# Softmax normalised in front of the transposes instead of behind the context, in a fused attention and feed-forward kernel

## The chip, the core and the metric

The kernel runs on one core of a Trainium2 chip, in one launch. The metric is the device time of that launch in microseconds. A core has five engines that run side by side, each with its own in-order instruction queue: TensorE (PE; its weight loads, PEld, overlap its matmuls), VectorE (DVE), ScalarE (ACT), GpSimd (POOL) and SyncE (SP, which here only issues DMAs). They meet at semaphores. TensorE writes to PSUM, the accumulation memory; everything else lies in SBUF.

## The reference

The whole computation has four layers over 8 batches of a 512 x 512 array: a step of a partial differential equation on a grid, a transformer block with adaptive layer norm, an expert feed-forward layer, and a gated low-rank response. The change lies in the attention of the transformer block. With B = 8, S = 512, 16 heads of 32 columns, and float32 throughout:

```python
x = _ln(src) * (1.0 + scale) + shift          # src: result of the grid step
q = (x @ Wq + bq)   # and k, v alike, split into 16 heads of 32
scores = einsum('bhqd,bhkd->bhqk', q / sqrt(32), k) + attention_bias
scores = where(src_mask, -inf, scores)
probs = softmax(scores, axis=-1)
ctx = einsum('bhqk,bhkd->bhqd', probs, v)
x = x + (ctx @ Wo + bo)
h = _ln(x) * g2 + beta2
x = x + _gelu2(h @ W1 + b1) @ W2 + b2
```

The bias is a full array of 8 x 16 x 512 x 512 values, 134 MB, and is read once.

## The kernel before

The kernel has three stages. `grid_stage` does the grid step of batch 0 and prepares coefficients. `attention_stage` does the attention of all 8 batches and, spread through it, the grid step of batches 1 to 7. `mlp_stage` does the rest; it begins near 1,110 us. The change touches `attention_stage` alone.

**Units.** The attention is cut into 128 units (b, c, r): batch b, group c of four heads, and r, one of four sets of 128 query rows. Within a batch I write t = 4c + r, from 0 to 15. A unit has four score tiles of 128 queries x 512 keys, one for each of its heads, and two bias tiles `bt` of two heads each (index u = 0 for heads 0 and 1, u = 1 for heads 2 and 3). The bias tiles come from memory three units ahead (`load_bias`), GpSimd adds the mask to them one unit ahead (`add_mask`), and the softmax is done in place in them. So a `bt` tile holds first the bias, then the negated scores, then the exponentials.

**What one pass of the loop does.** In pass i three units are in flight: `now` = unit i, `old` = unit i-1, `two` = unit i-2.

- `scores(i)` was issued at the end of pass i-1: four matmuls into four PSUM tiles s0 to s3, one buffer each.
- `values(two)` runs in passes where the unit two back has odd r: probabilities transposed earlier (`pt`), times v, into `ctx`. So it stands in front of the transposes of units with even t.
- For u = 0 and 1: `turned(old, u)` transposes two heads of the unit before, four 128 x 128 blocks each, into PSUM tiles `tr`, of which there are two, and copies each out as `pt`, on VectorE or ScalarE by a list written out by hand (`early`). Then `softmax(now, u)`: VectorE joins score and bias, negated, and takes the row minimum `mn` in one instruction, and ScalarE makes the exponential with the row sum in `sums`. Then one step of a job.
- Jobs (`fill`) are the projections of q, k, v and o, the transposes of the normalised input (`x1_in`) and back (`x1_back`), and the conversion of masks. For t = 0, 4, 8, 11 the job is a q block, for 1, 5, 9, 13 a k block, for 2, 3, 6, 7 an o block, for 10, 12, 14, 15 a v block. q and o are moved out of PSUM by VectorE, k and v by ScalarE.
- After the jobs are drained, `divide` follows in every fourth pass (t = 1, 5, 9, 13 of the running unit), then `inverse(old)`, then the grid sums of this pass and their loads, then `scores(i+1)`.

**The division before.** `inverse(old)` takes the reciprocals of four row sums (`rs`, 128 x 4) and spreads each over 32 columns on ScalarE (`rw`, 128 x 128). Once four units of a head group are through, `divide` transposes the four `rw` on TensorE (`rb`), ScalarE moves that to SBUF (`rbs`), and VectorE multiplies the context by it on its way out of PSUM (`ct`).

**The grid sums.** VectorE does up to three sums or products of 128 x 1024 per pass, by a table written out by hand (`GRID`); a `|` in it parts what comes ahead of `divide` from what comes behind. `grid_gate` makes GpSimd wait, at the start of the next pass, for the last grid operation on VectorE before it adds the next mask.

**Order.** Nearly every instruction is emitted under `keep_in_program_order` (`pin`), so that each engine's queue has the order of the emitting code. An instruction that waits holds up all that stands behind it on its engine.

Of the kernel before, what the change touches and what calls it, by code (L numbers as in the profile page):

```python
# [11 lines left out]
F32 = mybir.dt.float32  # L12
# [4 lines left out]
ALU = mybir.AluOpType  # L17
# [4 lines left out]
S = 512  # L22
D = 512
P = 128
R = 4
NH = 16
HD = 32
# [517 lines left out]
def attention_stage(  # L545
# [12 lines left out]
    nc = tc.nc  # L558
    with ExitStack() as ctx:
        wp = ctx.enter_context(tc.tile_pool(name="aw", bufs=1, reuse_waits="tile"))  # L560
        pp = ctx.enter_context(tc.tile_pool(name="ap", bufs=2, reuse_waits="tile"))
        ps = ctx.enter_context(tc.tile_pool(name="a_ps", bufs=1, space=PSUM, reuse_waits="tile"))

        pin = tc.keep_in_program_order
# [4 lines left out]
        def tp(out, src):  # L569
            pin(nc.tensor.transpose(out, src, ident))  # L570
# [20 lines left out]
        def mask_out(b, r):  # L591
            m = pp.tile([P, S], BF16, name=f"mk_{b}_{r}", tag=f"mk{r}", bufs=1)
            pin(nc.scalar.activation(m, mask[b, r], AF.Copy, scale=NEG))
            mask[b, r] = m

        def load_mask(b, r):
            mask_in(b, r)
            mask_out(b, r)
# [16 lines left out]
        def x1_back(b, r):  # L615
            tr = ps.tile([P, KC, P], F32, name=f"xb_{b}_{r}", tag="tr", bufs=2)
            for c in range(KC):
                tp(tr[:, c, :], x1s[b, c][:, r::R])
            pin(
                nc.vector.tensor_tensor(  # L620
                    xt[b][:, r, :], tr.rearrange("p c f -> p (c f)"), bo, ALU.add
                )
            )
# [43 lines left out]
        def v_block(b, m, tag="m", bufs=1):  # L667
            pr = ps.tile([P, D], F32, name=f"pv_{b}_{m}", tag=tag, bufs=bufs)
            half = block(
                pr,  # L670
                lambda k: x1s[b, k][:, m * P : (m + 1) * P],
                lambda k: w["Wv"][:, k, :],
            )
            yield half(0)
            yield half(1)
            t = io.tile([P, D], F32, name=f"v_{b}_{m}", tag=f"v{m}", bufs=2)
            pin(nc.scalar.copy(t, pr))
            vs[b, m] = t
# [155 lines left out]
        def grid_sums(n, j, late=True, early=True):  # L834
            ops = GRID.get(j, "")
            if "|" in ops and not (late and early):
                ops = ops.split("|")[late]
            elif not late:
                ops = ""
            for op in ops.replace("|", "").split():  # L840
                if op == "hh":
                    grid_ghosts(n)
                else:
                    grid_op(n, op)
# [7 lines left out]
        def grid_step(i, f):  # L852
            for n in range(1, NB):
                j = i - (16 * (n - 1) - 8)
                if -2 <= j <= 16:
                    f(n, j)
# [50 lines left out]
        def grid_early(j):  # L907
            grid_sums(1, j)
            grid_loads(1, j)

        def fill(b, t):

            n = b + 1
            jobs = []
            if b == 0:
                if t == 0:
                    homes = (("m", 1), ("tr", 2), ("tr", 2), ("ctx", 1))
                    for m in range(4):
                        jobs.append(v_block(0, m, *homes[m]))
                        jobs.append(grid_early(j) for j in (m + 3,))  # L920
                    jobs.append(grid_early(7) for _ in range(1))
                    jobs.append(mask_out(0, r) for r in (2, 3))
                elif t == 2:
                    jobs.append(add_bv() for _ in range(1))
                elif t in (3, 4, 7, 8):
                    jobs.append(x1_back(0, (3, 4, 7, 8).index(t)) for _ in range(1))
            if n == NB:
                at = dict(q=(0, 4, 9), k=(1, 6, 10), o=(2, 3, 7, 8))
                for key, f in (("q", q_block), ("k", k_block)):
                    if t in at[key]:  # L930
                        jobs.append(f(b, at[key].index(t) + 1))
                if t in at["o"]:
                    jobs.append(o_block(b - 1, at["o"].index(t)))
            elif t in (0, 4, 8):
                jobs.append(q_block(b, t // 4 + 1))
            elif t in (1, 5, 9):
                turn = (lambda c: x1_in(n, c)) if t == 9 else None
                jobs.append(k_block(b, t // 4 + 1, turn=turn))
            elif t in (2, 3, 6, 7):
                if b:  # L940
                    jobs.append(o_block(b - 1, (2, 3, 6, 7).index(t)))
            elif t == 11:
                jobs.append(q_block(n, 0))
            elif t == 13:
                jobs.append(k_block(n, 0))
            else:
                jobs.append(v_block(n, (10, 12, 14, 15).index(t)))
            if n < NB:
                if t in (11, 12, 13, 14):
                    jobs.append(x1_back(n, t - 11) for _ in range(1))  # L950
                if t >= 12:
                    jobs.append(load_mask(n, t - 12) for _ in range(1))
            elif t == 8:
                jobs.append(head_stats() for _ in range(1))
            elif t in (10, 11):
                jobs.append(head_norm(r) for r in (2 * t - 20, 2 * t - 19))
            elif t >= 12:
                jobs.append(head_turn(t - 12) for _ in range(1))
            for j in jobs:
                yield from j  # L960


        bias, ss, sums = {}, {}, {}
        pts, ctxs = {}, {}
# [86 lines left out]
                        k == 0, k == KC - 1,  # L1051
                    )

        def inverse(b, c, r):
            rs = small.tile([P, 4], F32, name=f"rs_{b}_{c}_{r}", tag="rs")
            pin(nc.vector.reciprocal(rs, sums.pop((b, c, r))))
            rw = pp.tile([P, 4, HD], F32, name=f"rw_{b}_{c}_{r}", tag="rw", bufs=4)
            pin(nc.scalar.copy(rw, rs[:, :, None].to_broadcast([P, 4, HD])))
            sums["w", b, c, r] = rw

        def divide(b, c):
            rb = ps.tile([P, R, P], F32, name=f"rb_{b}_{c}", tag="tr", bufs=2)
            for r in range(R):
                tp(rb[:, r, :], sums.pop(("w", b, c, r)).rearrange("p h d -> p (h d)"))
            rbs = pp.tile([P, S], F32, name=f"rbs_{b}_{c}", tag="rbs", bufs=1)
            pin(nc.scalar.copy(rbs, rb.rearrange("f r p -> f (r p)")))
            ct = pp.tile([P, S], F32, name=f"ct_{b}_{c}", tag="ct", bufs=5)
            pin(
                nc.vector.tensor_tensor(
                    ct, ctxs.pop((b, c)).rearrange("f r p -> f (r p)"), rbs, ALU.mult  # L1070
                )
            )
            cts[b, c] = ct

        def drain(jobs):
            for _ in jobs:
                pass
# [28 lines left out]
        for i in range(n + 2):  # L1106
            now = units[i] if i < n else None
            old = units[i - 1] if 1 <= i <= n else None
            two = units[i - 2] if i >= 2 else None
            jobs = fill(now[0], 4 * now[1] + now[2]) if now else iter(())  # L1110
            grid_gate(i)
            if i + 1 < n:
                add_mask(*units[i + 1])
            grid_step(i - 1, grid_pow)
            pair = two and two[2] % 2 == 1
            if pair:
                values(two[0], two[1], two[2] // 2)
            for u in range(2):
                if old:
                    turned(*old, u)  # L1120
                if now:
                    softmax(*now, u)
                next(jobs, None)
            drain(jobs)
            split = pair and two[2] == R - 1
            if split:
                grid_step(i, lambda n, j: grid_sums(n, j, late=False))
                divide(two[0], two[1])
            if old:
                inverse(*old)  # L1130
            if i + 3 < n:
                load_bias(*units[i + 3])
            if now and now[0] == NB - 1:
                head_load(4 * now[1] + now[2])
            if now and now[0] and now[1:] == (2, 1):
                nc.sync.dma_start(x1d[now[0] - 1], xt[now[0] - 1])
            grid_step(i, lambda n, j: grid_sums(n, j, early=not split))
            grid_step(i, grid_loads)
            if i + 1 < n:
                scores(*units[i + 1])  # L1140
# [821 lines left out]
```

## Time and profile before

| | |
|---|---|
| time, median of 3 runs | 2741.48 us (2741.33 to 2741.9) |
| the profiled execution | 2742.26 us, its span 2740.5 us |
| mean granted TensorE clock in the span | 0.994 |
| PE busy in the span | 2697.7 us (98%) |
| DVE, ACT, POOL busy in the span | 1910.8, 1030.4, 1501.5 us |
| one attention batch of 16 units (batches 1 to 6) | 125.8 us |
| ACT: one exponential of 128 x 512 | 715 ns |
| POOL: one mask addition of 128 x 1024 | 2141 ns |
| `rb` transposes on PE, 128 of them | 273 ns each (median) |
| `rw` and `rbs` copies on ACT | 297 and 570 ns (medians) |

A line of the timeline in the profile gives the start in us from the span's start, the length, the engine, the line of the kernel, the operation, the tiles written and read (out<-in, buffer numbers left out), the shape, and how many such instructions were put together (x4). Square brackets at its end tell how long the engine stood idle before it and what ended that. A line of a group of instructions gives the busy time, the mean duration in ns, and the idle time before them. L567 and L570 are the helpers `mm` and `tp`, through which all matmuls and transposes of this stage go; so they are told apart by their tiles. Matmuls overlap one another, so the durations of single ones add up to more than the time they take.

### The profile page before, as it was taken

The page shows a single profiled execution, that of the slowest core. Times are in us where ns is not written, and L with a number is a line of the kernel's source. Part 1 is how long each engine was busy: PE and PEld are TensorE (multiplying, and loading weights), DVE is VectorE, ACT ScalarE, POOL GpSimd, SP SyncE. Part 2 cuts the span into 40 slices and gives each one's busy share as a digit, 9 for nine tenths or more (in the row PEclk, how much of TensorE's full clock was granted, in tenths as well). Part 3 has the DMA queues.
Part 4 walks back from the last instruction along what each step waited for, and adds up shares of the span by engine and source line. Part 5 has one row for each costly group of instructions (what it writes and reads, how often), then busy time and mean ns, then how long its engine had stood idle before and what let it go on. Part 6 is the DMA issues. An engine that isn't in the chain of part 4 may idle for free.

```text
span 2740.5 us, 39851 instructions
## 1 busy us (share of the span) xinstructions
PE 2697.7 (98%) x14662; PEld 2008.0 (73%) x14662; DVE 1910.8 (70%) x3514; ACT 1030.4 (38%) x2189; POOL 1501.5 (55%) x1090
## 2 busy tenths in 40 slices
PE   7999999999999999999999999999999999999998
PEld 4455555555555555788888888888888888888887
DVE  7888888888888756577656756655456566565665
ACT  2566776766676766211211211211121221221221
POOL 3455555555555653565566555655636546546543
PEclk9999999999999999999999999999999999999999
DMA  8765767666676554642533443353133143142120
GB/s 314 241 204 178 242 188 239 204 217 222 196 235 192 166 156 158 192 123 41 161 127 73 124 144 100 79 163 118 58 127 116 58 158 116 59 158 100 58 77 31
DMA packets 190208, 405.27 MB, mean 148 GB/s; under 512 B 24024, under 2 KB 28704, under 8 KB 183742
## 3 DMA queue, kind: packets, MB, share of 16 engines
q1 hardware_dynamic: 186202, 391.97, 42.8%
q0 software_dynamic: 3360, 10.68, 3.1%
q8 instruction: 117, 1.92, 0.3%
q14 instruction: 77, 0.63, 0.1%
q10 hardware_dynamic: 452, 0.07, 0.0%
HBM read 366.97 MB, written 31.50 MB: 145 GB/s over the span
## 4 chain that ended last, share of the span: by engine, by line
PE 95%; DVE 3%; DMA 1%; issue 0%; ACT 0%; SPq 0%; ACTq 0%; POOL 0%; DVEq 0%; POOLq 0%
PE u L1177 28%; PE y L1177 28%; PE tr L570 8%; PE s L567 6%; PE ctx L567 4%; PE o L567 4%; PE pq L567 4%; PE pk L567 4%; PE pv L567 4%; PE btr L1180 1%; PE l L251 1%; DVE bt L1005 1%; PE rb L570 1%; PE xb L570 1%; PE ytr L1180 1%; DMA a<-in_A 0%
## 5 line engine op out<-in xcount | busy, mean ns | idle before, releaser
L982 POOL TENSOR_TENSOR bt<-bt,mk 128x1024 f32<-128x1024 f32 x256 | 542.6, 2141 | 56.8 <-DMA bt<-in_bias 47.3
L1177 PE MATMUL y<-wo,act 128*128 128x256 f32 x2560 | 572.8, 380 | 0.0
L1177 PEld LDWEIGHTS y<-wo,act 128*128 128x128 f32 x2560 | 481.5, 190 | 69.9 <-issue 6.7
L1010 ACT ACTIVATE bt<-bt,mn 128x512 f32<-128x512 f32 x512 | 365.6, 715 | 84.0 <-DVE mn L1005 83.1
L570 PEld LDWEIGHTS tr<-ident,bt 128*128 128x128 f32 x2048 | 228.7, 141 | 147.1 <-issue 114.1
L1005 DVE CUSTOM_DVE_ANT_0 bt<-s,bt 128x512 f32<-128x512 f32 x512 | 330.7, 683 | 1.3 <-PE s L567 1.3
L1177 PE MATMUL u<-bt,wi 128*128 128x256 f32 x1440 | 330.5, 379 | 0.0
L1183 DVE TENSOR_TENSOR act<-u,u 128x512 f32<-128x512 f32 x256 | 173.2, 686 | 210.3 <-PE u L1177 132.6
L1177 PEld LDWEIGHTS u<-bt,wi 128*128 128x128 f32 x1440 | 273.5, 190 | 37.2
L570 PE MATMUL tr<-ident,bt 128*128 128x128 f32 x2048 | 275.5, 277 | 7.5 <-ACT pt L1037 4.1
L1177 PE MATMUL u<-tb,ws 128*128 128x256 f32 x1024 | 242.2, 379 | 0.0
L1177 PE MATMUL y<-t,s 128*128 128x256 f32 x1024 | 234.2, 380 | 0.0
L1037 ACT COPY pt<-tr 128x512 f32<-128x512 f32 x306 | 172.8, 581 | 156.1 <-PE tr L570 152.8
L1186 POOL TENSOR_TENSOR t<-wo,t 128x512 f32<-128x512 f32 x64 | 106.6, 1682 | 200.5 <-PE y L1177 200.5
L1035 DVE COPY pt<-tr 128x512 f32<-128x512 f32 x206 | 141.7, 688 | 105.4 <-PE tr L570 97.1
L1177 PEld LDWEIGHTS u<-tb,ws 128*128 128x128 f32 x1024 | 194.3, 190 | 26.6 <-DVE tb L1183 0.2
L1177 PEld LDWEIGHTS y<-t,s 128*128 128x128 f32 x1024 | 191.1, 190 | 24.1
L1497 ACT ACTIVATE act<-act,b 128x512 f32<-128x512 f32 x128 | 82.9, 711 | 293.0 <-DVE act L1183 293.0
L1497 ACT ACTIVATE act<-act,bi 128x512 f32<-128x512 f32 x128 | 83.8, 712 | 282.6 <-DVE act L1183 282.6
L1183 DVE TENSOR_TENSOR x<-y,x 128x512 f32<-128x512 f32 (+1 forms) x97 | 64.6, 679 | 161.2 <-PE y L1177 107.3
L567 PE MATMUL s<-kt,qt 32*128 32x512 f32 x1024 | 173.7, 643 | 3.4 <-DVE mn L1005 2.5
L1183 DVE TENSOR_TENSOR u<-u,u 128x512 f32<-128x512 f32 x192 | 131.1, 683 | 57.9 <-PE u L1177 57.8
(325 smaller groups left out, 4252.3 us busy)
## 6 DMA issues: line engine op xcount, KB each, us to landing
bt<-in_bias SPq DMA_DIRECT2D x256, 512.0 KB
wo<-in_W SPq DMA_DIRECT2D x32, 1024.0 KB
wi<-in_Wi SPq DMA_DIRECT2D x32, 1024.0 KB
wo<-in_Wo_e SPq DMA_DIRECT2D x32, 1024.0 KB
wi<-in_W SPq DMA_DIRECT2D x28, 1024.0 KB
gq<-coef_q SPq DMA_DIRECT2D x21, 512.0 KB
x1d<-x SPq DMA_DIRECT2D x8, 1024.0 KB
x<-x1d SPq DMA_DIRECT2D x8, 1024.0 KB
```

Of the source, the lines that this page charges most:

```text
L567: pin(nc.tensor.matmul(out, lhsT=lhsT, rhs=rhs, start=start, stop=stop))
L570: pin(nc.tensor.transpose(out, src, ident))
L982: nc.gpsimd.tensor_tensor(bt, bt, mask[b, r][:, None, :].to_broadcast([P, 2, S]), ALU.add)
L1005: nc.vector.tensor_tensor_reduce(bt[:, i, :], ss[h], bt[:, i, :], -1.0, 3.0e38, ALU.add, ALU.min, mn)
L1010: nc.scalar.activation(bt[:, i, :], bt[:, i, :], AF.Exp, bias=mn, scale=-1.0, accum_out=sums[b, c, r][:, h : h + 1],)
L1035: pin(nc.vector.tensor_copy(pt[:, :, r % 2, :], tr))
L1037: pin(nc.scalar.copy(pt[:, :, r % 2, :], tr))
L1177: pin(nc.tensor.matmul(out, lhsT=lhsT, rhs=rhs, start=start, stop=stop))
L1180: pin(nc.tensor.transpose(out, src, idn))
L1183: pin(nc.vector.tensor_tensor(out, x, y, op))
L1186: pin(nc.gpsimd.tensor_tensor(out, x, y, op))
L1497: nc.scalar.activation(acts[g][:, k, :], acts[g][:, k, :], func, bias=bi[:, j : j + 1])
```

## The change

The row sums are applied to the exponentials themselves, in place, before they are transposed. `inverse` is called twice per unit, for heads 0 and 1 and for heads 2 and 3, now for the running unit `now` and no longer for `old`: the first call right behind the drained jobs, the second behind the grid sums. Each call makes the reciprocal of two sums on VectorE, multiplies the first of the two heads on ScalarE (128 x 512, a scale per row), and the second on GpSimd (128 x 512). `divide` becomes `context`: the transposes `rb`, the copies `rw` and `rbs` and the product are gone, and VectorE copies the context out of PSUM as it is. Apart from this, the four jobs of batch 0 that turn the normalised input back (`x1_back`) come at t = 3, 4, 6 and 7 in place of 3, 4, 7 and 8.

```diff
@@ fill
-                elif t in (3, 4, 7, 8):
-                    jobs.append(x1_back(0, (3, 4, 7, 8).index(t)) for _ in range(1))
+                elif t in (3, 4, 6, 7):
+                    jobs.append(x1_back(0, (3, 4, 6, 7).index(t)) for _ in range(1))
@@ attention_stage
-        def inverse(b, c, r):
-            rs = small.tile([P, 4], F32, name=f"rs_{b}_{c}_{r}", tag="rs")
-            pin(nc.vector.reciprocal(rs, sums.pop((b, c, r))))
-            rw = pp.tile([P, 4, HD], F32, name=f"rw_{b}_{c}_{r}", tag="rw", bufs=4)
-            pin(nc.scalar.copy(rw, rs[:, :, None].to_broadcast([P, 4, HD])))
-            sums["w", b, c, r] = rw
-
-        def divide(b, c):
-            rb = ps.tile([P, R, P], F32, name=f"rb_{b}_{c}", tag="tr", bufs=2)
-            for r in range(R):
-                tp(rb[:, r, :], sums.pop(("w", b, c, r)).rearrange("p h d -> p (h d)"))
-            rbs = pp.tile([P, S], F32, name=f"rbs_{b}_{c}", tag="rbs", bufs=1)
-            pin(nc.scalar.copy(rbs, rb.rearrange("f r p -> f (r p)")))
+        def inverse(b, c, r, u):
+
+            rs = small.tile([P, 2], F32, name=f"rs_{b}_{c}_{r}_{u}", tag="rs")
+            pin(nc.vector.reciprocal(rs, sums[b, c, r][:, 2 * u : 2 * u + 2]))
+            bt = bias[b, c, r, u]
+            pin(nc.scalar.mul(bt[:, 0, :], bt[:, 0, :], rs[:, 0:1]))
+            pin(nc.gpsimd.tensor_scalar(bt[:, 1, :], bt[:, 1, :], rs[:, 1:2], None, ALU.mult))
+
+        def context(b, c):
             ct = pp.tile([P, S], F32, name=f"ct_{b}_{c}", tag="ct", bufs=5)
-            pin(
-                nc.vector.tensor_tensor(
-                    ct, ctxs.pop((b, c)).rearrange("f r p -> f (r p)"), rbs, ALU.mult
-                )
-            )
+            pin(nc.vector.tensor_copy(ct, ctxs.pop((b, c)).rearrange("f r p -> f (r p)")))
             cts[b, c] = ct
@@ the loop
             drain(jobs)
+            if now:
+                inverse(*now, 0)
             split = pair and two[2] == R - 1
             if split:
                 grid_step(i, lambda n, j: grid_sums(n, j, late=False))
-                divide(two[0], two[1])
-            if old:
-                inverse(*old)
+                context(two[0], two[1])
             if i + 3 < n:
                 load_bias(*units[i + 3])
...
             grid_step(i, lambda n, j: grid_sums(n, j, early=not split))
+            if now:
+                inverse(*now, 1)
             grid_step(i, grid_loads)
```

## The prediction

> **What bounds the kernel now.** I read the page's chain first, then busy time by stage, then the timeline at one hand-over between units.
>
> ```profile
> PE 95%; DVE 3%; DMA 1%; issue 0%; ACT 0%; SPq 0%; ACTq 0%; POOL 0%; DVEq 0%; POOLq 0%
> ...
> 217.33:343.10 125.77, 125.53 (x818) 69.19 (x817) 110.37 (x238) 87.09 (x207) 71.63 (x51) 1.00 0.66 211
> 343.10:468.87 125.77, 125.52 (x817) 69.18 (x816) 109.75 (x237) 87.56 (x209) 71.68 (x51) 1.00 0.65 212
> ```
>
> The chain is TensorE. The stretches are two batches of attention, 16 units each (columns: length, then busy time of PE, weight loads, DVE, ACT, POOL, then the clock, DMA share and rate). Batches 1 to 6 repeat alike and PE is busy for all but 0.25 us: fewer PE instructions shorten a batch, and any wait put before PE lengthens it. ACT and POOL have room in sum, DVE less. So it matters when each result is there. Unit t=1 hands over to t=2:
>
> ```profile
> 357.55 1.22 DVE L695 TENSOR_TENSOR x<-x,gf 128x1024 f32<-128x1024 f32 x1
> 357.68 0.60 PE L570 MATMUL rb<-ident,rw 128*128 128x128 f32 x4
> 357.77 0.71 ACT L1010 ACTIVATE bt<-bt,mn 128x512 f32<-128x512 f32 x1
> 358.21 1.14 PE L567 MATMUL s<-kt,qt 32*128 32x512 f32 x8
> 358.48 0.67 ACT L661 ACTIVATE kt<-pk,bqk 128x512 f32<-128x512 f32 x1
> 359.05 0.57 ACT L1066 COPY rbs<-rb 128x512 f32<-128x512 f32 x1
> 359.28 1.09 PE L570 MATMUL tr<-ident,bt 128*128 128x128 f32 x8
> 359.65 0.69 DVE L1069 TENSOR_TENSOR ct<-ctx,rbs 128x512 f32<-128x512 f32 x1 [0.88 <-ACT rbs L1066]
> 360.67 1.07 ACT L1037 COPY pt<-tr 128x512 f32<-128x512 f32 x2
> 361.93 1.04 PE L570 MATMUL tr<-ident,bt 128*128 128x128 f32 x8
> ```
>
> PE issues the scores of unit 2 (s) and 1.07 us later the transposes (tr) of unit 1's heads 0 and 1. Their exponentials are long done, but ACT is still on the unit's last one. After an even unit the values (ctx) come between, and the transposes start 2.94 after the scores. Heads 2 and 3 follow at 3.72 (odd) or 5.58 (even).
>
> **The change, part by part.** *Removed:* 128 rb transposes; four stream in 0.44 us (unit t=1 takes 8.71, the like unit t=15 without rb 8.27), so 32 x 0.44 = 14 us of PE's path. ACT loses 128 rw copies (0.29) and 32 rbs copies (0.57), 55 us beside PE. The context copy stays at 0.69 on DVE, without its 0.88 wait.
>
> *Added, in sums:* 128 more reciprocals (two small ones per unit, some 0.09 each in DVE's queue, 11 us of its slack); 256 multiplies on ACT at the exponential's 0.72, 184 us, which makes 103 of 126 in a batch; 256 on POOL. All would hide by busy time.
>
> POOL's price has no like row:
>
> ```profile
> L1186 POOL TENSOR_TENSOR ws<-w 128x512 f32<-128x512 f32 x3 | 3.8, 1274 | 0.1
> L319 POOL COPY zi<-ident 128x128 f32<-128x128 f32 x1 | 0.3, 292 | 0.1
> L320 POOL TENSOR_SCALAR zi<-ident 128x128 f32<-128x128 f32 x1 | 0.6, 562 | 0.0
> ```
>
> The copy carried to 512 columns gives 0.6, the tensor_scalar 1.57; the two-input form at the right size is 1.27. The Trainium skill, "GPSIMD Engine Reference", section 3.1, puts a tight loop over 512 elements at 769 ns. I take 0.9, below the two-input row since one operand less is read, and keep 0.6 and 1.57: 29 us a batch on POOL, 101 of 126.
>
> *Waits, heads 0 and 1.* The first `inverse` stands behind the drained jobs, so ACT's multiply of head 0 queues behind the last exponential and behind what jobs leave on ACT (kt, v, mask). At t=1: kt is through at 359.05, the multiply ends at 359.77, PE sees it some 0.15 later (mn to s shows 0.14 to 0.18): 359.92 in place of 359.28, though PE, without rb, would be ready at 358.84. At t=3 the reciprocal waits for DVE's add of o (start 0.71 after the scores), the multiply runs 0.91 to 1.63, PE starts at 1.78 in place of 1.07. At t=15 v and mask go first: 345.65 for 344.17. After even units the 1.87 us of values cover all this; without that cover it would cost the like again.
>
> *Head 1 and the shared port.* The grid sums stand right behind the reciprocal on DVE, with both inputs in SBUF:
>
> ```profile
> 362.96 4.23 POOL L982 TENSOR_TENSOR bt<-bt,mk 128x1024 f32<-128x1024 f32 x2
> 366.32 1.95 DVE L695 TENSOR_TENSOR x<-x,gc 128x1024 f32<-128x1024 f32 x1
> ```
>
> This one takes 1.95 in place of 1.22, as if it began when POOL ended (367.19). So DVE's first sum (1.1) goes ahead of POOL's multiply, and the multiply ahead of the second sum: at t=3 POOL runs 1.9 to 2.8, and PE, wanting head 1 at 2.2, waits 0.7 more.
>
> *Heads 2 and 3.* The second reciprocal is behind all grid sums. ACT's multiply of head 2 waits for it, and the evictions of heads 0 and 1 (pt) are queued behind that multiply; PE needs their two PSUM buffers for heads 2 and 3. Where DVE evicts head 0 instead, that copy stood behind the grid sums before too and loses nothing but the port's time. At t=1: sums and reciprocal done at 362.2, multiply to 362.9, eviction to 363.5, so PE gets its buffer at 363.65; it wanted it at 362.53. At t=3 this adds 0.4.
>
> *Given back.* At t=2 and 6 DVE is 1.13 late for the next scores now (eight scores matmuls spread over 2.28 in place of 1.14); a PE that is already late hides that.
>
> *Net per unit, the saving of rb included.* t=1 and 5: heads 2 and 3 start 1.72 late, which covers DVE's 1.13, so 0.56 each remains. t=3: 0.71 (head 0) + 0.72 (head 1) + 0.4 (buffer) = 1.85. t=7: DVE has statistics there, [...]so only POOL's mask add (to 1.21) is in the way: 0.71 + 0.04 + 0.25 = 1.0. t=9: the last exponential ends 2.16 ahead of the scores, heads 0 and 1 come in time, and the buffers cost 0.55. t=11: one sum only, 0.71 + 0.72 = 1.4. t=13: kt and mask on ACT put PE's start from 329.02 to 329.72, POOL adds 0.35: 1.05. t=15: 1.5. Even units: 0. Sum 8.5 a batch, 51 for batches 1 to 6. Batch 7 has no grid sums (no port wait), and PE is idle there for 7.3 us of 125 already, which takes up a part: 4. Batch 0 is uneven, with DVE late in it: 4, guessed from the others' half. Total +59. With POOL at 0.6 the units 3, 11 and 13 lose some 0.8: 7.7 a batch, +54. At 1.57 heads 1 and 3 are 0.67 later at the seven odd units up to t=13: 13.2 a batch, +93 with the end batches in step.
>
> *The rest.* The add of the mask moves behind POOL's two multiplies: about 1 later, where the next unit reads it 1.5 to 6 later; at 1.57 that cover wears through at places. relu and its row transfer on ACT's queue come at most 0.72 later, and nothing waits for them before the next grid step. Bias loads on SP keep their order, three units ahead, and wait for buffers as late as PE itself is. Batch 0's turns (8 transposes and two adds moved one unit ahead, no DMA): t=8 has a 1.8 gap in front of one now, t=7 is tight itself; -3 to +2, I take 0.
>
> *The clock.*
>
> ```profile
> 92.50:95.90 3.40, 2.00 (x5) 0.68 (x4) 3.37 (x7) 1.48 (x2) 0.67 (x2) 1.00 1.04 400
> 133.40:136.80 3.40, 1.50 (x13) 1.04 (x11) 3.40 (x7) 1.31 (x4) 0.60 (x2) 1.00 0.43 120
> 136.80:143.60 6.80, 6.80 (x32) 3.15 (x36) 6.73 (x12) 3.97 (x11) 3.76 (x2) 0.50 0.29 97
> ```
>
> The Trainium skill, "TensorE: Matmul & The Clock Gate", Part 1, lets the clock halve after an idle window of about 3.4 us; by it these stalls cost nothing more. The trace is stricter: 1.50 busy of 3.40 was followed by half clock, 2.00 was not. My stalls leave PE 1.9 to 2.4 of 3.4 in their windows (t=15: 3.4 - 1.5; t=3: 3.4 - 1.43), between the two or above, and a stall is often split over two windows. I take 0; a halved window costs 1.7, three a batch over seven batches 36.
>
> **Sum.** The profiled execution took 2742.3 (span 2740.5 and 1.8 around it), 0.8 above the median 2741.5. 2742.3 + 59 - 0.8 = 2800.
>
> **Rivals.** (1) Everything hides: the multiplies reach PE before 1.07. Then rb's 14 goes, and some of the 18 of t=2 and 6: 2715 to 2727, faster. For it: room on ACT and POOL, sums of heads 0 and 1 ready 1 to 3 us ahead. Against: the order on ACT. It would need head 0's multiply to end by 0.9 after the scores, that is to stand before the last exponential, which the code doesn't do: 0.05. (2) The waits only eat the saving, within 5 of 2741: 0.03. (3) Waits half of mine, POOL not held by the port: 6 to 40, near 2765: 0.10. (4) My forecast, 40 to 75: 0.50. (5) POOL at 1.57, or half clock: heads 1 and 3 become the last, 93 in all, with the clock's 36 near 130: 2816 to 2870. For it: the only tensor_scalar row of POOL; against: that is one row, beside small sums of DVE: 0.32.
>
> A measurement here tells 0.2% (5.5 us) from no change. Faster 0.05, same 0.03, slower 0.92. The range leaves out (1), (2) and the ends: 2762 to 2868.
>
> **What would show it.** PE instructions 128 fewer; PE idle in front of tr, released by ACT bt and POOL bt, at odd units and not at even ones; batches of 134 in place of 125.8; POOL's multiply often near 2 by the port; clock 1.00. Wrong: batches under 126, or waits at even units, or halved clock throughout.

## The result, and the profile after

| | before | after |
|---|---|---|
| median of four runs each, side by side | 2741.69 us (2741.33 to 2744.88) | 2964.6 us (2959.65 to 2966.65) |
| the profiled execution, and its span | 2742.26, 2740.5 us | 2962.91, 2961.1 us |
| mean granted TensorE clock in the span | 0.994 | 0.970 |
| one attention batch, batches 1 to 5 | 125.8 us | 155.6 and 158.4 us, in turn |
| batch 6 | 125.8 us | 149.5 us |

The ratio is 1.0809, interval 1.0796 to 1.0822: 223 us slower. The forecast was 2800, with 2762 to 2868 around it. The direction was right and the size was not. Batches 1 to 6 make 178 of the 223, batch 0 makes 23 and batch 7 makes 19.

The page of the changed kernel, its busy times and its chain by engine:

```profile
PE 2757.7 (93%) x14534; PEld 2019.1 (68%) x14534; DVE 1964.3 (66%) x3642; ACT 1148.0 (39%) x2285; POOL 2012.7 (68%) x1346
...
PE 73%; POOL 12%; DVE 8%; issue 4%; ACT 2%; DMA 1%; SPq 0%; ACTq 0%; POOLq 0%; DVEq 0%
```

PE has 128 instructions fewer (14,534 for 14,662), as the rb transposes are gone; it is nevertheless busy 60 us longer, which the slower clock does: without POOL's multiplies (an experiment below, clock 0.992) the same instructions keep it busy 2682.1 us. In the chain POOL has gone from 0 to 12%, DVE from 3 to 8%. ACT, which got as many multiplies as POOL, has 2%.

Two batches in busy time by stage (columns: length, then busy PE, weight loads, DVE, ACT, POOL, then clock, DMA share and rate):

```profile
240.50:396.13 155.63, 132.55 (x801) 69.60 (x800) 118.19 (x254) 101.82 (x220) 138.38 (x84) 0.95 0.53 171
396.13:554.53 158.40, 135.31 (x801) 70.29 (x801) 117.61 (x253) 102.03 (x221) 138.37 (x84) 0.94 0.52 168
```

PE stands idle 23 us of every batch, where it was 0.25. POOL is busy 138.4, where the forecast put 101. Its multiply in the groups of 240 to 1130 us (busy time, mean ns, then the idle time before it and what ended it):

```profile
L1060 POOL TENSOR_SCALAR bt<-bt,rs 128x512 f32<-128x512 f32 x182 | 371.5, 2045 | 103.1 <-DVE rs L1057 102.8 <-DVE gsh L817 0.3
```

From the list of waits in 240 to 1150 us (us in total, times, longest; the lines between, of DVE and ACT, are left out):

```profile
PEld tr L570 <- POOL bt L1060: 115.2, 83, 4.3
POOL bt L1060 <- DVE rs L1057: 105.5, 96, 3.1
...
PE tr L570 <- POOL bt L1060: 95.0, 61, 4.0
PEld tr L570 <- ACT bt L1059: 88.9, 70, 2.2
```

POOL's multiply waits for its reciprocal 102.8 us in 5.7 batches, 18 a batch. 138.4 and 18 are 156: POOL works or waits for DVE in the whole of a batch. The page's average of 68% busy does not tell that; in a batch it is 88%. POOL has become the engine that sets the pace, and PE waits for its multiplies most.

The hand-over that was shown before, unit t=1 to t=2, now in batch 2 (the timeline; lines of other tiles left out):

```profile
409.49 1.57 POOL L1060 TENSOR_SCALAR bt<-bt,rs 128x512 f32<-128x512 f32 x1 [1.58 <-DVE rs L1057]
...
411.02 0.19 POOL L744 TENSOR_TENSOR gate<-gq 128x1 f32<-128x1 f32 x1
...
411.16 5.21 POOL L982 TENSOR_TENSOR bt<-bt,mk 128x1024 f32<-128x1024 f32 x2
...
413.03 0.16 DVE L1057 RECIPROCAL rs<-sums 128x2 f32<-128x2 f32 x1
...
413.41 1.14 PE L567 MATMUL s<-kt,qt 32*128 32x512 f32 x8
...
414.91 2.54 DVE L695 TENSOR_TENSOR gq<-gq,gq 128x1024 f32<-128x1024 f32 x1
...
415.31 0.66 PE L570 MATMUL tr<-ident,bt 128*128 128x128 f32 x4 [0.75 <-ACT bt L1059]
...
416.35 5.12 POOL L1060 TENSOR_SCALAR bt<-bt,rs 128x512 f32<-128x512 f32 x2
...
417.38 1.21 DVE L695 TENSOR_TENSOR gc<-gc,gf 128x1024 f32<-128x1024 f32 x1
...
418.51 0.15 DVE L1057 RECIPROCAL rs<-sums 128x2 f32<-128x2 f32 x1
...
419.99 1.11 PE L570 MATMUL tr<-ident,bt 128*128 128x128 f32 x4 [4.03 <-POOL bt L1060]
```

Read it along POOL. The multiply of unit 0's head 3 waits 1.58 for the second reciprocal and runs until 411.06. Behind it come the gate and the two mask additions, until 416.37. Only then can POOL begin on head 1 of unit 1, whose reciprocal has lain ready since 413.19. DVE's sum gq was held until POOL's mask additions ended (2.54 for 1.2), and the next sum gc goes ahead too; POOL's multiply of head 1, the first of the two in its line, gets through behind both, near 420, after about 3.6 us. PE did head 0 at 415.31, 1.90 after the scores, and head 1 at 419.99, 6.58 after them, in place of 1.56.

### The profile page after: what moved, and what is told of

Read it like the earlier page. It is cut to its first block, busy times and chain, and to the rows that moved or that the text cites. A ratio compares the mean times of both kernels' runs of the same rounds, so it can differ in the third digit from the quotient of the medians.

```text
span 2961.1 us, 40235 instructions
## 1 busy us (share of the span) xinstructions
PE 2757.7 (93%) x14534; PEld 2019.1 (68%) x14534; DVE 1964.3 (66%) x3642; ACT 1148.0 (39%) x2285; POOL 2012.7 (68%) x1346
## 4 chain that ended last, share of the span: by engine, by line
PE 73%; POOL 12%; DVE 8%; issue 4%; ACT 2%; DMA 1%; SPq 0%; ACTq 0%; POOLq 0%; DVEq 0%
PE u L1171 26%; PE y L1171 26%; POOL bt L1060 6%; PE tr L570 5%; POOL bt L982 5%; PE o L567 3%; PE pv L567 3%; PE pq L567 2%; DVE x L695 2%; PE pk L567 2%; PE ctx L567 1%; PE btr L1174 1%; PE l L251 1%; PE s L567 1%; DVE x L796 1%
## 5 line engine op out<-in xcount | busy, mean ns | idle before, releaser
L1060 POOL TENSOR_SCALAR bt<-bt,rs 128x512 f32<-128x512 f32 x256 | 505.3, 1979 | 148.2 <-DVE rs L1057 137.7
L570 PEld LDWEIGHTS tr<-ident,bt 128*128 128x128 f32 x2048 | 244.8, 149 | 359.0 <-POOL bt L1060 137.8
L570 PE MATMUL tr<-ident,bt 128*128 128x128 f32 x2048 | 321.9, 295 | 173.8 <-POOL bt L1060 113.3
L1059 ACT ACTIVATE bt<-bt,rs 128x512 f32<-128x512 f32 x256 | 181.5, 717 | 193.2 <-DVE rs L1057 189.8
```

The source lines that it names most:

```text
L1059: pin(nc.scalar.mul(bt[:, 0, :], bt[:, 0, :], rs[:, 0:1]))
L1060: pin(nc.gpsimd.tensor_scalar(bt[:, 1, :], bt[:, 1, :], rs[:, 1:2], None, ALU.mult))
```

## The experiments

All are edits of the changed kernel, unless said. The question after the result: of 223 us, how much is ACT's, how much is POOL's, and of POOL's, is it the price of the multiply, the port (what GpSimd and DVE hold each other up when both read SBUF), the wait, or the clock?

**The turns of batch 0 alone** (an edit of the kernel before).

```diff
-                elif t in (3, 4, 7, 8):
-                    jobs.append(x1_back(0, (3, 4, 7, 8).index(t)) for _ in range(1))
+                elif t in (3, 4, 6, 7):
+                    jobs.append(x1_back(0, (3, 4, 6, 7).index(t)) for _ in range(1))
```

> The kernel before with only batch 0's turns moved to 3, 4, 6, 7. Taken as 0 in the forecast: -3 to +2 us. If the last turn at t=8 was what made PE idle and halved its clock there: -3 to -5.

2740.5 us, ratio 0.9992 (0.9983 to 1.0). Batch 0 goes from 145.4 to 141.1, batch 7 (up to its last transposes) from 117.8 to 121.1, and the two together change by 1.0. The turns are no part of the loss.

**Without the multiplies; without POOL's; without ACT's.**

```diff
-            pin(nc.scalar.mul(bt[:, 0, :], bt[:, 0, :], rs[:, 0:1]))                                  # e3, e2
-            pin(nc.gpsimd.tensor_scalar(bt[:, 1, :], bt[:, 1, :], rs[:, 1:2], None, ALU.mult))        # e3, e1
```

> The changed kernel without any multiply (nothing is divided); the reciprocals, the plain copy of the context and the missing rb transposes stay. Both theories: the saving alone, 14 us of rb, and between 0 and 18 of VectorE's lateness at t=2 and 6: 2709 to 2728. If it stays above 2741, the smaller parts (256 reciprocals, the turns of batch 0) cost something too.

> The changed kernel without GpSimd's multiplies: heads 1 and 3 stay undivided, and ScalarE still divides heads 0 and 2. Theory G (GpSimd's multiply is the cause: 1.56 us each in front of the mask addition, and held up by the grid sums on VectorE): most of the 223 us goes; what stays is ScalarE's order (some 5 to 6 us a batch at odd units): 2770 to 2800. Rival A (the order on ScalarE and VectorE, last exponential and grid sums ahead of the multiplies, makes the transposes late whoever multiplies): above 2900.

> The changed kernel without ScalarE's multiplies: heads 0 and 2 stay undivided, and GpSimd still divides heads 1 and 3. Theory G: nearly the whole loss stays, 2880 to 2950. Rival A: most of it goes, 2760 to 2800.

| | median, us | ratio to before |
|---|---|---|
| no multiplies (e3) | 2719.59 | 0.9914 (0.9897 to 0.993) |
| ACT's alone (e1) | 2794.55 | 1.0187 (1.017 to 1.0204) |
| POOL's alone (e2) | 2955.22 | 1.0771 (1.0753 to 1.0789) |
| both (the change) | 2964.6 | 1.0809 (1.0796 to 1.0822) |

What the change takes away is worth 22 us (24 against the kernel before measured beside it; batches of 122.7). ACT's multiplies then cost 75, and POOL's a further 170. The two do not add up from the other side: with POOL's in place, ACT's cost only 9, and batches 1 to 6 are as long without them (155.7 and 158.4 in turn, then 149.4). I had expected at most 2950 for POOL's alone. Whichever is later decides, and that is POOL. Without POOL's multiplies the chain is PE's again:

```profile
PE 87%; DVE 6%; issue 2%; ACT 2%; DMA 1%; POOL 1%; SPq 0%; ACTq 0%; POOLq 0%; DVEq 0%
```

**ACT's order.** The first reciprocal and ACT's multiply of head 0 go in front of the last exponential of the unit. POOL's multiplies are left out, so this is compared with ACT's alone.

```diff
@@ softmax, behind the exponential
+                if u == 1 and i == 0:
+                    inverse(b, c, r, 0)
@@ the loop
             drain(jobs)
-            if now:
-                inverse(*now, 0)
```

> The changed kernel without GpSimd's multiplies (2794 in the earlier run) and with the first reciprocal and ScalarE's multiply of head 0 moved between the last two exponentials; heads 1 and 3 stay undivided. Theory A0 (ScalarE's order ahead of heads 0 and 1 makes most of the 75 us between that run and the one without multiplies): 2745 to 2770. Rival A2 (it is the second reciprocal behind the grid sums, with the evictions queued behind head 2's multiply): 2780 to 2800.

2759.65 us, 1.0071 (1.0054 to 1.0088): 35 of ACT's 75 us go. In the trace head 0's transposes start 1.07 after the scores at every odd t of batches 1 to 4, the value of before; with ACT's multiply behind the last exponential they started at 1.64 to 2.52. What remains is behind the second reciprocal. The waits of PE in 240 to 1090 us in this kernel begin with

```profile
PE tr L570 <- ACT pt L1039: 29.7, 23, 1.9
```

that is, head 2 waits for the PSUM buffer that ACT's eviction (pt) gives back, and the eviction is queued behind the multiply of head 2. Heads 2 and 3 started 3.72 after the scores before; here they start at 5.37 at t=1 and 5, at 4.51 at t=3, and at 5.74 at t=7.

**POOL: price.** The multiply covers 256 of the 512 columns, so the other 256 columns of heads 1 and 3 are left undivided.

```diff
-            pin(nc.gpsimd.tensor_scalar(bt[:, 1, :], bt[:, 1, :], rs[:, 1:2], None, ALU.mult))
+            pin(nc.gpsimd.tensor_scalar(bt[:, 1, 0:256], bt[:, 1, 0:256], rs[:, 1:2], None, ALU.mult))
```

> The changed kernel with GpSimd multiplying only 256 of 512 columns of heads 1 and 3 (the other half stays undivided). By the two rows of GpSimd's multiply (1.56 us for 512 columns, 0.23 fixed) that is 0.9 us, the price the forecast was made with. Theory G1 (the price alone made the forecast fall short, the rest of the working holds): 2790 to 2815. Theory G2 (GpSimd is behind for other reasons too: its queue and the port): 2830 to 2890.

2850.07 us, 1.0393 (1.0377 to 1.0409). The tile view of rs gives the multiply's min, median and max in ns, first of the changed kernel, then of this one:

```profile
L1060 POOL TENSOR_SCALAR bt<-bt,rs x256: 1554/1564/3698, 92.6 to 1308.2; 128x512 f32<-128x512 f32 x128
```

```profile
L1060 POOL TENSOR_SCALAR bt<-bt,rs x256: 915/923/3057, 92.7 to 1191.7; 128x256 f32<-128x256 f32 x128
```

This is the forecast's own price, as the edit was meant to make it: 0.92 where it took 0.9. At that price the kernel still takes 2850, not 2800. So of the 165 us between forecast and result some 115 go with the price and what follows from it, and some 50 were missing even at the price of the forecast. The maxima show a second thing: a multiply can be held up by more than 2 us.

**POOL: neither wait nor reading.** Three memsets of 128 x 512 replace the multiply; they last as long as it, but do not read and do not wait for the reciprocal. Heads 1 and 3 get a constant.

```diff
-            pin(nc.gpsimd.tensor_scalar(bt[:, 1, :], bt[:, 1, :], rs[:, 1:2], None, ALU.mult))
+            for _ in range(3):
+                pin(nc.gpsimd.memset(bt[:, 1, :], 0.002))
```

> The changed kernel with GpSimd's multiply replaced by three memsets of the same 128x512 (heads 1 and 3 hold a constant): about as long on GpSimd (some 1.5 us together), but nothing is read. Theory P (a good part of the loss comes from the port: GpSimd held up by the grid sums, 1.98 us on average against 1.56 alone, and the sums by GpSimd): 2850 to 2910. Rival (the time on GpSimd decides, whoever shares a port): 2935 to 2970.

2791.79 us, 1.0175 (1.016 to 1.0191), which is the time without POOL's multiplies. Its POOL groups in 240 to 1130:

```profile
L982 POOL TENSOR_TENSOR bt<-bt,mk 128x1024 f32<-128x1024 f32 x218 | 461.4, 2139 | 0.2 <-issue 0.2
...
L1061 POOL MEMSET bt<- 128x512 f32 x651 | 337.5, 526 | 33.9 <-ACT bt L1010 9.0
```

Three of 526 ns are 1.58 us of POOL per head, and they cost nothing, though POOL is busy for 121 of the 131 us of a batch. Neither of my expectations had this: both put a cost on the time that POOL works. Busy time on POOL alone is not what hurts.

**POOL: the wait, without reading.** The same three memsets, but in front of them a memset of one column of rs, which has to wait until DVE has written rs; or, second, an addition of that column to itself, which waits alike and reads.

```diff
+            pin(nc.gpsimd.memset(rs[:, 1:2], 1.0))                              # e17
+            pin(nc.gpsimd.tensor_tensor(g, rs[:, 1:2], rs[:, 1:2], ALU.add))    # e9, g a tile of one column
             for _ in range(3):
                 pin(nc.gpsimd.memset(bt[:, 1, :], 0.002))
```

> As the run with memsets behind a one-column addition (2922), but the instruction that waits for the reciprocal is a memset over the reciprocal's own column, so it waits for VectorE and reads nothing; in that run the one-column addition took 543 ns on average against 194 for such an addition elsewhere, so it still met the port. Heads 1 and 3 hold a constant. Theory P (the port, now gone): 2792 to 2825. Theory W (the wait for the reciprocal, with the mask addition and the next multiply queued behind it): 2890 to 2930. Between, in parts.

> As the run with memsets, but each group of memsets stands behind a GpSimd addition of one column (0.19 us) that reads the reciprocal, so GpSimd waits for VectorE as the changed kernel does; heads 1 and 3 still hold a constant. The run without it took 2792, but had lost that wait too. Theory P (the port): 2792 to 2815. Theory W (the wait for a reciprocal behind VectorE's sums, with GpSimd's queue behind it): 2900 to 2965.

The first takes 2882.77 us, 1.0515 (1.0499 to 1.0531); the second 2922.46, 1.0654 (1.0636 to 1.0672). POOL's groups in 240 to 1130, of the first and then of the second:

```profile
L982 POOL TENSOR_TENSOR bt<-bt,mk 128x1024 f32<-128x1024 f32 x199 | 437.5, 2220 | 0.0
L1062 POOL MEMSET bt<- 128x512 f32 x597 | 312.6, 525 | 22.9
...
L1060 POOL MEMSET rs<- 128x1 f32 x199 | 19.6, 99 | 86.8 <-DVE rs L1057 86.0
```

```profile
L1061 POOL TENSOR_TENSOR gw<-rs 128x1 f32<-128x1 f32 x192 | 104.2, 543 | 49.8 <-DVE rs L1057 44.6 <-DVE x L695 4.7
```

The memsets last as in the run without the wait, 525 ns; new in the first is that POOL stands still for 86 us until rs is there, and that the mask additions and the next unit's work stand behind that. It costs 91 us (2882.8 less 2791.8), of which the 0.1 us of the extra memset can be a small part. This is 7 us less than I had expected of the wait alone; the second run lies within its range.

The 91 us are not free of the port, though. The mask additions read, and when the wait pushes them back they meet DVE's sums. One of the sums in 240 to 1130, first with the memsets alone, then with the wait in front of them:

```profile
L695 DVE TENSOR_TENSOR gq<-gq,gq 128x1024 f32<-128x1024 f32 x10 | 12.2, 1215 | 0.0
```

```profile
L695 DVE TENSOR_TENSOR gq<-gq,gq 128x1024 f32<-128x1024 f32 x11 | 21.4, 1945 | 0.0
```

All sums of 128 x 1024 in batches 1 to 6 take 147 us in place of 128. By the order of the code a longer sum makes the second reciprocal later, and with it the end of POOL's next wait; how much of the 91 this makes was not separated. From there to the changed kernel it is 82 more, and the difference is that POOL's own work for the two heads now reads next to DVE's sums. Even a reading of one column costs 40 of these: it lasts 543 ns, where the gate, a like operation of one column, lasts 193.

**POOL: head 3 alone, head 1 alone** (with ACT's multiplies).

```diff
+            if u:          # e13: head 3 alone; e14: "if not u", head 1 alone
                 pin(nc.gpsimd.tensor_scalar(bt[:, 1, :], bt[:, 1, :], rs[:, 1:2], None, ALU.mult))
```

> The changed kernel with GpSimd multiplying head 3 alone (head 1 stays undivided). Without both it took 2794, with both 2965. If the second multiply, behind all grid sums and in front of the next mask addition, is what matters: 2850 to 2900, more than the other one alone. If it only meets a later need than head 1: 2800 to 2830.

> The changed kernel with GpSimd multiplying head 1 alone (head 3 stays undivided). If the second multiply is what pushes the mask addition, and through it the next first one: 2800 to 2840. If head 1 is late by itself, held by the sums in the port: 2860 to 2900.

2841.34 us, 1.036 (1.0345 to 1.0376), and 2874.05, 1.0481 (1.0465 to 1.0497). The multiply in 240 to 1090 of the two:

```profile
L1061 POOL TENSOR_SCALAR bt<-bt,rs 128x512 f32<-128x512 f32 x98 | 153.3, 1564 | 232.1 <-DVE rs L1057 232.1
```

```profile
L1061 POOL TENSOR_SCALAR bt<-bt,rs 128x512 f32<-128x512 f32 x96 | 241.8, 2519 | 139.0 <-DVE rs L1057 121.1 <-DVE x L695 10.6 <-DVE gsh L817 7.3
```

Head 3's multiply comes behind all sums of its pass and is never held: 1564 ns on the mean. It costs 47 us over ACT's alone, with POOL idle 232 us for its reciprocal. Head 1's comes beside the sums, lasts 2519 on the mean, and costs 80. I had expected the second multiply, head 3's, to cost more than head 1's; it costs less. Together they cost 170 and not 127: one unit's head 3, the mask addition and the next unit's head 1 make one chain on POOL, as in the timeline above, and each lateness is passed on to the next.

**The clock.** Matmuls whose product is overwritten fill PE's stall in front of head 1's transposes: first generously, then fitted.

```diff
@@ turned, in front of the transposes
+                if u == 0 and i == 1:    # e8 also: and 1 <= b <= 6, with {1: 4, 5: 4, 3: 2, 11: 1, 12: 1}
+                    for _ in range({1: 8, 5: 8, 3: 5, 11: 3, 12: 2, 9: 1, 13: 1, 15: 1}.get(t, 0)):
+                        mm(tr.rearrange("p k q -> p (k q)"), ident, w["Wo"][:, 0, :], True, True)
```

> The changed kernel with 1 to 8 extra matmuls of 128x512 (0.43 us each, overwritten by the transposes behind them) in front of head 1's transposes, at the units where PE stands idle there, no more than the idle time holds. Theory C (the idle stretches halve PE's clock for the next window, and that is a third of the loss: 154 us at half clock in attention against 10 before): the halved windows at t=2, 4, 6 and 12 go, 2895 to 2930. Rival (half clock falls on work that would wait for GpSimd anyway): 2955 to 2975, with as few halved windows.

2996.15 us, 1.0923 (1.0905 to 1.0942): a miss. The clock is back at 0.992, but I had put too many in: one such matmul is two instructions and takes 0.86 us, so eight of them outlast the stall of about 5 us. Batches 1 to 5 take 156.7, no less than before the filling (157.0 on the mean), and batch 7, which has hardly any such stalls, takes 145.6 in place of 123.3 for its first 15 units.

> The changed kernel with extra matmuls in front of head 1's transposes in batches 1 to 6 alone, half as many as in the run before (one takes 0.86 us and not 0.43, so that run overfilled the idle time): 4 at t=1 and 5, 2 at t=3, 1 at t=11 and 12. Theory C (half clock costs by itself): each batch some 7 us shorter, 2915 to 2935. Rival (GpSimd's queue holds PE either way): 2955 to 2975.

2924.27 us, 1.0657 (1.0641 to 1.0673), clock 0.986. The same stretch as the first batch shown above:

```profile
240.50:396.13 155.63, 141.72 (x846) 72.08 (x844) 122.64 (x262) 106.48 (x230) 143.72 (x88) 0.99 0.55 180
```

Adding work to PE makes the kernel 40 us faster. The time at half clock within the attention falls from 153.6 to 54.6 us (10.2 in the kernel before). So some 40 of the 223 are the clock's, for two thirds of the halved time. They lie within the 170, not beside them: POOL's stalls make them.

**A version that could beat the kernel before.** First, the early order with both POOL multiplies. Second, the early order with head 1 alone on POOL, head 3 on ACT, and the second reciprocal moved ahead, behind the first grid operation of the pass. Third, as the second, but head 1 on ACT too at t = 2, 5, 6 and 7.

```diff
@@ inverse, second and third version
-            pin(nc.gpsimd.tensor_scalar(bt[:, 1, :], bt[:, 1, :], rs[:, 1:2], None, ALU.mult))
+            if u:          # third: "if u or 4 * c + r in (2, 5, 6, 7):"
+                pin(nc.scalar.mul(bt[:, 1, :], bt[:, 1, :], rs[:, 1:2]))
+            else:
+                pin(nc.gpsimd.tensor_scalar(bt[:, 1, :], bt[:, 1, :], rs[:, 1:2], None, ALU.mult))
```

> The changed kernel with the whole first call of inverse (reciprocal, ScalarE's head 0, GpSimd's head 1) moved between the last two exponentials; the second call stays behind the grid sums. Theory P (the port): head 1 runs ahead of the sums and is no longer held, head 3 still is: 2830 to 2890. Theory Q (GpSimd simply has too much to do, two multiplies and a mask addition a unit): 2900 to 2965.

> A rebuilt order, with everything divided: the first reciprocal, ScalarE's multiply of head 0 and GpSimd's of head 1 between the last two exponentials; the second reciprocal behind the first grid operation, and ScalarE multiplying heads 2 and 3, so GpSimd has one multiply a unit, started ahead of the sums. If order and port are the whole cause, it comes near the run without multiplies (2720): 2730 to 2760. If ScalarE (some 115 of 123 us a batch then) or the mask addition in front of head 1 holds it: 2770 to 2830.

> The rebuilt order (2758) with head 1 given to ScalarE at t = 2, 5, 6 and 7, where GpSimd's mask addition ended too late for it (head 1's transposes 1 us late at t=5 and 7). If only that was left: some 2 us a batch less, 2738 to 2748, level with the kernel before. If ScalarE is then the one that is late: 2755 to 2775.

2923.96 us (1.0663, 1.0645 to 1.0681), 2758.3 (1.0057, 1.004 to 1.0073) and 2762.49 (1.0076, 1.0063 to 1.009). With both multiplies on POOL the better order gives 41 us and POOL still decides. If holding by the sums were all, it would have come to 2830 to 2890; but head 1's multiply still stands behind the late mask addition, and at t=1 head 1 still starts 6.57 after the scores in five of the six batches 1 to 6. The second version does every division and loses only 0.6%, 206 us less than the change. Its POOL multiply, in 240 to 1090:

```profile
L1070 POOL TENSOR_SCALAR bt<-bt,rs 128x512 f32<-128x512 f32 x108 | 194.8, 1803 | 36.0 <-DVE rs L1064 35.4
```

POOL, with one multiply per unit, now waits 36 us for reciprocals in place of some 100. The time is near that of the early order without any POOL multiply (2759.65), but that run keeps the second reciprocal behind all sums, so this does not show that the multiply on POOL is free: head 1 starts 1.0 late at t=5 and 1.1 late at t=7, released by POOL. The third version takes these two away, as meant, but is no faster: at t=7 heads 2 and 3 then start 5.40 after the scores, where the second version had 4.87 and the kernel before 3.72. None of these beats the kernel before, and what is missing was not taken apart further.

## Why the prediction was wrong in size

The account by medians, each step beside the forecast's:

| step | forecast | measured |
|---|---|---|
| rb gone, and some of t=2 and 6 | 14, and some of 18 | 22 (e3) |
| ACT's multiplies: a batch, against the kernel before | 125.8 + 8.5 - 1.8 = 132.5 us | 131.95 us (e1) |
| POOL: 1.5 us of work per head by itself | 0 | 0 (e6) |
| POOL: waiting, with its queue behind | 0 | about 90 (e17; it includes what the late mask additions and DVE's sums cost each other) |
| POOL: its work for the two heads reading beside DVE's sums | about 1.8 us a batch | about 80 (after less e17) |
| clock, within the last two rows | 0 | some 40 (e8) |
| turns of batch 0 | 0 | 0 (e7) |

**Right.** The saving; the turns; and ACT's share, to half a microsecond in a batch. That the sum comes so near is in part luck: by the lengths of the units, the step of t=7 was 1.1 too small, and those of t=1, 5 and 9 together 1.3 too large. The single times of head 0 agree: without POOL's multiplies head 0 starts 2.09 after the scores at t=1 (forecast 2.15: the 359.92 less scores that come 0.44 earlier, at 357.77), 1.73 at t=3 (1.78) and 2.52 at t=15 (2.55, from 345.65 in the same way). Heads 2 and 3 start 5.37 after the scores at t=1, where the forecast's 363.65 makes 5.88. At t=7 they start at 5.75 in place of 3.72, 2.03 late, for which the forecast's steps had 1.0 in all. "Given back" holds in full: without POOL's multiplies the transposes of t=2 and 6 start at 2.94 and no longer at 4.07. That these stalls lie at odd t was right for heads 0; head 1 came late at t=10 and 12 also, by 0.6 and 1.1.

**Wrong, first: "The add of the mask moves behind POOL's two multiplies: about 1 later, where the next unit reads it 1.5 to 6 later".** I held the mask addition's end against its reader only. I did not ask what stands behind it in POOL's queue: the next unit's first multiply, for which PE waits 1.56 after the scores. In the kernel before, the mask addition for unit t=2 was this one:

```profile
355.33 2.14 POOL L982 TENSOR_TENSOR bt<-bt,mk 128x1024 f32<-128x1024 f32 x1
```

It ended at 357.47, 0.74 ahead of the scores at 358.21. In the changed kernel it ends at 416.37, 2.96 after the scores at 413.41: 3.7 later, and the multiply begins there. The rule that stands in the description of the kernel, that a waiting instruction holds up all that stands behind it, was applied to ACT and to DVE, and not to POOL. This is the step that fails at any price. The forecast put POOL's waiting at nothing, and it costs about 90 at the length of work that the chip has (e17). At the price that I had taken 50 us are missing (e5), which this step, the next one and the clock share; how they share them was not measured.

**Second: "DVE's first sum (1.1) goes ahead of POOL's multiply, and the multiply ahead of the second sum".** In the timeline two sums go ahead. Of 256 multiplies 86 took over 2 us and 29 over 3. The Trainium skill, "SBUF — State Buffer", section "SBUF: two separate sides", has a lock that a VectorE operation with two SBUF inputs takes only against a GpSimd operation that reads, and that is held for the whole instruction. The runs agree: memsets stay at 525 to 526 ns, the reading of one column goes from 193 to 543. But that GpSimd loses to a second sum although it has waited since before the first ended is what this trace adds; I had taken a fair turn. Nor did I count the other direction: the mask addition, pushed beside the sums, holds them in its turn (2.54 for 1.2 in the timeline).

**Third: the price, 0.9 for 1.56.** I put it below the two-input row "since one operand less is read". The one like row of the profile had given 1.57. The Trainium skill's 769 ns ("GPSIMD Engine Reference", section 3.1) pulled me away from it, but that section speaks of the best case of a tight unrolled loop; here the measurement decides, 1.56. With it I had the rival (5), and it would still have fallen short: it added 0.67 per head at seven units, when POOL's loop passes each delay to the next unit.

**Fourth: the clock, "I take 0; a halved window costs 1.7".** The stalls were sized too small (6.58 for head 1 at t=1), so PE's windows are emptier than the forecast's 1.9 to 2.4 of 3.4. Windows of the changed kernel in pairs, a window and the next:

```profile
536.09:539.50 3.41, 1.73 (x16) 0.83 (x9) 3.29 (x7) 2.29 (x4) 2.84 (x2) 1.00 0.29 102
539.50:542.91 3.41, 3.41 (x7) 1.43 (x6) 0.81 (x4) 2.00 (x5) 3.41 (x4) 0.50 0.38 100
...
416.59:420.00 3.41, 0.01 (x1) 0.01 (x1) 3.28 (x7) 1.19 (x2) 3.41 (x2) 1.00 0.01 2
420.00:423.41 3.41, 3.41 (x7) 1.91 (x8) 0.00 (x0) 2.00 (x5) 3.41 (x3) 0.50 0.24 52
```

The window of 0.01 fits the Trainium skill ("TensorE: Matmul & The Clock Gate", Part 1: an idle window lets the clock halve); the one of 1.73 does not, since PE is half busy in it. Of the 33 steps to half clock between 72 and 1310 us, 7 follow a window with PE busy for 4% or less, 19 one of 18 to 36%, and the others one of half or more; so by the rule alone most would not have come. The bound that the trace of before showed, between 1.50 and 2.00 of 3.40, was the one to use, with stalls of the right size; three windows of about 1.6 were not followed by half clock, and of six windows with PE busy for 51% three were and three were not, so it is not sharp, and something besides the busy share decides. What that is stays open.

The forecast gave 0.92 to slower, and its range ended at 2868, because it added up the uncertain costs as if each were paid once per unit.

## What to carry to other kernels

When an engine is given work that waits, write down its whole queue over one turn of the loop, with the wait in it, and compare the length of that turn with the period: busy time in sum (101 of 126) says nothing if 18 us of waiting come on top and each delay is handed on. Check a moved instruction not only against its own reader but against the reader of what stands behind it. Give GpSimd work that neither waits for VectorE nor reads beside its sums, as the memsets here, or work that nobody awaits; an operation there that reads SBUF beside VectorE's two-input sums must be counted at its own price plus a run of such sums, and a stall of PE of half a clock window must be counted with the clock.

## What the runs showed of the hardware

- GpSimd's tensor_scalar with a scale per row takes 1.56 us for 128 x 512 (median of 256), more than the 1.27 of the two-input tensor_tensor of 128 x 512 that the forecast showed, and 0.92 for 128 x 256.
- A GpSimd multiply that is ready can lose to two VectorE sums in a row: up to 3.70 us for 1.56. Memsets on GpSimd of the same total length keep their 526 ns each beside the same sums. The other way round, a mask addition that GpSimd has begun holds a VectorE sum: 2.54 us for 1.2 in the timeline.
- Half clock follows windows of 3.41 us in which PE was busy for a third or even, in some cases, for half, not idle ones alone; filler matmuls in the stalls gave 40 us back.
